# Moving the sums of the spectra's squares from VectorE to GpSimd, and the store and spread load of the sampling offsets to later steps

## The chip, the cores and the metric

The kernel runs on one core of a Trainium2 chip. The metric is the device time of one execution in microseconds (us); lower is better. The engines of the core are named as in the profile: PE (TensorE, matrix products; its weight loads are shown apart as PEld), DVE (VectorE), ACT (ScalarE), POOL (GpSimd) and SP (SyncE, which here only issues transfers). Each of them runs its own instructions in order and waits for the others by semaphores. DMA transfers are issued from the queues of SP, ACT and POOL.

## The reference, cut to what matters

The input is 32 images of 96 channels, 56x56 pixels, float32. Two layers follow each other. The first expands 96 to 576 channels, runs a 3x3 depthwise convolution, weighs the channels by a squeeze and adds a projection back to 96. The second one is a deformable block, and the change lies in it:

```python
mag = jnp.abs(jnp.fft.rfft2(x, norm='ortho'))       # spectrum of the input, |.| per channel
...                                                   # channel weights ca and pixel weights sa from it
y = x * ca * sa
magy = jnp.abs(jnp.fft.rfft2(y, norm='ortho')).mean(1, keepdims=True)
freq_e = jax.image.resize(magy, (b, 1, h, w), method='bilinear')
aux = jnp.concatenate([y, coord, freq_e], 1)
offset = _conv(aux, off_w, off_b, (1, 1))             # 9 taps x (dx, dy) for each pixel
...
sampled = _grid_sample_taps(y, px, py)                # bilinear samples at the shifted places
y_def = jnp.einsum('bcthw,oct->bohw', sampled, def_w.reshape(c, c, 9))
```

So each image needs two spectra of 96 channels (of `x` and of `y`), and each pixel needs nine offsets that become weights of the sampling.

## The kernel before, in words

The first layer's output goes to DRAM image by image (`x1d`). Three pieces of work are interleaved by hand in `layers` and run at the same time for three images: `first(b + 2)`, the expansion and depthwise convolution (`hidden`, its taps are the L262 instructions of DVE); `second(b + 1)`, projection, spectra and attention (`attend`); and the deformable convolution of image b, which goes over seven bands of 8 rows (`NBD`, from L1120 on). `first` and `second` are generators. A band has 17 slots; in each slot `pump()` advances both generators as far as their share of the 119 slots of an image says, and beside it the generator `offsets` of the band after next is advanced by one `yield` for each of the 14 column tiles of the band. "A step" is one such `yield`.

**The spectra** are made by `dft_mag`, which `attend` calls twice for each image: once on `x` (the first spectrum; its resized mean is `fe`), once on `y` (the second; `fy`). In its last loop (L411 to L426) it goes over three groups of channels. For each group PE makes the real and imaginary parts in two PSUM banks (L420), ACT squares both into a tile `sq` of 128x2x2x232 (L423, two instructions), and DVE adds the squares of the two parts into the spectrum tile `s1` (L424, one instruction, 128x464). The pool `sq` has two buffers, so the squares of the third group need the sum of the first one to be done. After the three groups ACT takes the root of all of it in place (L427), and `resized_spectrum` reduces it over the channels on DVE (`m_fe` or `m_fy`, L437; for the second spectrum DVE first weighs it, L436), and PE multiplies that with a small matrix (L440).

**The offsets** are made by `offsets`, one call for each band, two bands ahead. PE convolves (`joint_conv`, L615), DVE copies the 18 offset rows out of PSUM into the tile `at` (L664), POOL stores `at` to a DRAM tile `od` (L668), SP loads `od` back, spread over 112 partitions, as `ht` (L680, 252 KB), and ACT turns `ht` into hat functions `ho` (L686 and L688), which go out to DRAM (`hd`, L690) and come back as the sampling weights `wc` and `wr` (L702, L703), which DVE multiplies (L709) and PE uses (L738). Between these, the base convolution of the band runs (L644), and DVE reduces `at` to the largest offset (L675).

**The order.** The instruction order of PE, ACT, DVE and POOL is made when the program is built, by a list scheduler that has its own estimate of the times and follows the order of the program text as priority. SP's queue is in the order of the program text (`manual_schedule`). An instruction given to `keep_in_program_order` is tied to its place in the text. Other transfers of SP's queue that matter here: `hq<-h2d` (L311, the rows of the first layer for the projection, 784 and 980 KB by turns; the projection's matmuls are L329), `hq<-x1d` (L369, rows for the spectra, twelve of 98 KB for each spectrum), `xt<-in_x` (L213) and `yp<-x1d` (L594). POOL also copies blocks of the image (`ybl`, L720, twice for each half band), weighs the rows for the second spectrum (L373), adds the residual (L476), and issues the transfers L317, L477, L571, L587, L596 and L1060. PE's other lines in what follows: L169 (expansion), L396 (first half of the transform), L724 (transposes of `ybl`), L757 (deformable convolution). The spectrum's rows are put into `s1` by ACT (L403); L649 and L173 are the evacuations of the base convolution and the expansion.

Of the kernel before, what the change touches and what calls it, by code (L numbers as in the profile page):

```python
# [7 lines left out]
FP = mybir.dt.float32  # L8
# [20 lines left out]
NOFF, NTAP = 18, 9  # L29
# [8 lines left out]
NTX = W // TS  # L38
NTH = NTX // 2
TP = TS * TS  # L40
# [22 lines left out]
NQB = 8  # L63
# [54 lines left out]
def bank(p):  # L118
    return p["mm"].tile([128, 512], FP, name="mm")
# [182 lines left out]
def project_rows(p, half):  # L302

    return p["hq"].tile([128, (NCH - 1, len(UNITS) - NCH + 1)[half], EW], FP, name=f"hq{half}")
# [39 lines left out]
def dft_mag(nc, p, src, gate=None):  # L344

    w = p["w"]
    hwc = src.rearrange("c (h w) -> h c w", h=H)
    s1 = p["s1p"].tile([2 * WX, NP, 2 * V], FP, name="s1")
    if gate is None:
        parts = p["sq"].tile([2 * WX, 2, NPB * V], FP, name="sq")[: 2 * H, :, : NG * W].rearrange("p k (g w) -> p k g w", g=NG)
    x2s = []
    for i in range(2):  # L360
        rows = project_rows(p, i).rearrange("p u n -> p (u n)")[: 2 * H, : NG // 2 * CG * WX].rearrange("h (c w) -> h c w", w=WX)
        nc.vector.memset(rows[:, :, W:], 0.0)
        x2s.extend(rows[:, g * CG : (g + 1) * CG] for g in range(NG // 2))

    def load(g):
        if g < NG:
            for half in range(2):
                c0 = half * C // 2 + g * CG
                nc.sync.dma_start(x2s[g][half * H : (half + 1) * H, :, :W], hwc[:, c0 : c0 + CG])  # L369

    def weigh(g):
        if gate is not None and g < NG:
            nc.gpsimd.tensor_tensor(x2s[g][:, :, :W], x2s[g][:, :, :W], gate.unsqueeze(1).to_broadcast([2 * H, CG, W]), ALU.mult)  # L373

    def sums(g):
        sq = bank(p)[: 2 * H, : CG * W].rearrange("h (c w) -> h c w", c=CG)
        nc.scalar.activation(sq, x2s[g][:, :, :W], AF.Square)
        for k, t in enumerate((x2s[g][:, :, :W], sq)):
            nc.vector.tensor_reduce(parts[:, k, g], t.rearrange("h c w -> h w c"), AX.X, ALU.add)

    if gate is None:
        yield
    for g in range(3):
        load(g)
    yield
    if gate is not None:
        yield
    weigh(0)
    weigh(1)
    yield  # L390
    if gate is not None:
        yield
    for g in range(NG):
        pt = bank(p)
        for i in range(CG // 2):
            nc.tensor.matmul(pt[:, i * 4 * V : (i + 1) * 4 * V],  # L396
                             x2s[g][:, 2 * i : 2 * i + 2, :].rearrange("h c w -> h (c w)"), w["FU"],
                             start=True, stop=True)
        if gate is None:
            sums(g)  # L400
        weigh(g + 2)
        load(g + 3)
        nc.scalar.copy(s1.rearrange("p (h q) u -> p h q u", h=2)[:, :, g * CG // 2 : (g + 1) * CG // 2],  # L403
                       pt[:, : 2 * CG * V].rearrange("p (q h u) -> p h q u", h=2, u=2 * V))
        yield
    if gate is None:
        p["sums"] = p["sp"].tile([2 * H, 2, W], FP, name="sums")
        nc.vector.tensor_reduce(p["sums"], parts.rearrange("p k g w -> p k w g"), AX.X, ALU.add)
    mag = s1[:, :, :V]
    n = NQB * V  # L410
    pairs = mag.rearrange("p (r q) u -> p r q u", r=2)  # L411
    for q0 in range(0, NP // 2, NQB):
        sq = p["sq"].tile([2 * WX, 2, 2, n], FP, name="sq")
        pts = bank(p), bank(p)
        for part, first, second in ((0, (0, 0), (1, V)), (1, (0, V), (2, 0))):
            for t, (g, u0) in enumerate((first, second)):
                for r, k in ((0, 0), (1, 1), (0, 1), (1, 0)):
                    rows = slice(r * WX, r * WX + W)
                    q1 = k * NP // 2 + q0
                    nc.tensor.matmul(pts[r][k * WX : (k + 1) * WX, part * n : (part + 1) * n].rearrange("p (q u) -> p q u", q=NQB),  # L420
                                     w["GV"][rows, g], s1[rows, q1 : q1 + NQB, u0 : u0 + V], start=(t == 0), stop=(t == 1))
        for r, pt in enumerate(pts):
            nc.scalar.activation(sq[:, r].rearrange("p k n -> p (k n)"), pt[:, : 2 * n], AF.Square)  # L423
        nc.vector.tensor_tensor(pairs[:, :, q0 : q0 + NQB], sq[:, :, 0].rearrange("p r (q u) -> p r q u", q=NQB),  # L424
                                sq[:, :, 1].rearrange("p r (q u) -> p r q u", q=NQB), ALU.add)
        yield  # L426
    nc.scalar.activation(mag, mag, AF.Sqrt)  # L427
    p["magnitude"] = mag
# [18 lines left out]
def attend(tc, p, b, x, h2d, pooled, x1, given=False):  # L447
# [32 lines left out]


    yield from dft_mag(nc, p, x1)
    mag = p["magnitude"]

# [89 lines left out]


    yield from dft_mag(nc, p, x1, sa)
    yield
    yield from resized_spectrum(nc, p, p["magnitude"], "fy", cx)
# [50 lines left out]
def joint_conv(nc, p, yp, j, hid):  # L629


    w = p["w"]
    pa = bank(p)
    conv3(nc, pa[:, :BW], w["joint"], yp, CJ, j)
    nc.scalar.activation(hid, pa[:DMID, :BW], AF.Relu, bias=w["dg1b"][:DMID])  # L635
    yb = p["yb"].tile([C, BW], FP, name="yb")
    nc.scalar.activation(yb[BC:], pa[OFF0 + QC :, :BW], AF.Identity, bias=w["cv"]("base_b")[BC:])
    yield yb, pa[OFF0 : OFF0 + NOFF, :BW]
    pb = bank(p)
    for k in range(NTAP):  # L640
        dy, dx = divmod(k, 3)
        r0 = j * RB + dy + PD - 1
        for i in range(2):
            nc.tensor.matmul(pb[i * BC : (i + 1) * BC, : BW // 2].rearrange("p (h w) -> p h w", h=RB // 2), w["base"][:, k],  # L644
                             yp[:C, r0 + i * RB // 2 : r0 + (i + 1) * RB // 2, dx + PD - 1 : dx + PD - 1 + W],
                             start=(k == 0), stop=(k == NTAP - 1))
    yield
    for i in range(2):
        nc.scalar.activation(yb[:BC, i * BW // 2 : (i + 1) * BW // 2], pb[i * BC : (i + 1) * BC, : BW // 2], AF.Identity,  # L649
                             bias=w["cv"]("base_b")[:BC])  # L650
    yield


def offsets(nc, p, yp, j, top, hid, ybs, hds, defer):

    w = p["w"]
    joint = joint_conv(nc, p, yp, j, hid)
    yb, pa = next(joint)  # L660
    ybs.append(yb)
    at = p["off"].tile([NOFF, NTX, 2, TP], FP, name="at")
    for s in range(2):
        nc.vector.tensor_copy(at[:, :, s].rearrange("o t (r c) -> o t r c", r=TS),  # L664
                              pa[:, s * BW // 2 : (s + 1) * BW // 2].rearrange("o (r t c) -> o t r c", r=TS, t=NTX))
    yield
    od = p["dp"].tile([NTX, 2, NOFF, TP], FP, name="od")
    nc.gpsimd.dma_start(od.rearrange("t s o p -> o (t s) p"), at.rearrange("o t s p -> o (t s) p"))  # L668
    yield
    next(joint)  # L670
    yield
    next(joint)
    yield
    next(joint, None)
    nc.vector.tensor_reduce(top, at.rearrange("o t s p -> o (t s p)"), AX.X, ALU.max, apply_absolute_value=True)  # L675
    for _ in range(4):
        yield
    ht = p["ht"].tile([SB * NTX, 4, KP], FP, name="ht")
    src = od.rearrange("t s o p -> t (s o p)").unsqueeze(0).to_broadcast([SB, NTX, 4 * KP])
    nc.sync.dma_start(ht.rearrange("q n k -> q (n k)"), src)  # L680
    for _ in range(6):
        yield

    def hats():
        ho = p["ht"].tile([SB * NTX, 2, 2, KP], FP, name="ho")
        p["tc"].keep_in_program_order(nc.scalar.activation(  # L686
            ho.rearrange("q x s n -> q s x n"), ht.rearrange("q (s x) n -> q s x n", s=2), AF.Abs, bias=w["blk"]))
        nc.scalar.activation(ho, ho, AF.Relu, bias=w["one"], scale=-1.0)  # L688
        hd = p["dp"].tile([2, 2, SB, NTX, KP], FP, name="hd")
        nc.scalar.dma_start(hd.rearrange("x s i t n -> (i t) (x s) n"), ho.rearrange("q x s n -> q (x s) n"))  # L690
        hds.append(hd)

    defer(hats)
# [259 lines left out]
def layers(tc, a, dp, x1d, zd, stats, far):  # L953
# [8 lines left out]
    with ExitStack() as ctx:  # L962
# [127 lines left out]
        def find(n):  # L1090
            if n % 2 == 0:
                hids.append(p["hid"].tile([2 * NS, BW], FP, name="hid"))
            hid = hids[n // 2][n % 2 * NS : n % 2 * NS + DMID]
            return offsets(nc, p, yp, bands[n][1], top[:, n % NBD : n % NBD + 1], hid, ybs, hds,
                           lambda hats: later.append((slot + 2, hats)))
# [420 lines left out]
```

## Time and profile before

| | us |
|---|---|
| three runs | 9002.55, 9001.68, 8979.61 |
| median | 9001.68 |
| the profiled execution | 8993.57 |
| its span, from the first to the last instruction | 8991.8 |
| PE busy, share of the span | 8180.0, 91% |
| DVE busy | 7174.8, 80% |
| ACT busy | 5380.8, 60% |
| POOL busy | 2600.4, 29% |
| mean granted clock of TensorE over the span | 0.940 |

How to read it: the first 450 us and the last 310 us hold the filling and the normalisation of the outputs; between them the profile repeats itself with one image every 263 us (the root L427 of the first spectrum starts at 3966.6 and the next one at 4229.5). Busy time is a sum over stages. PE's granted clock is either full or half in the records of this trace; a row of the window view gives its mean over a stretch. In the wait view a row names who waited, for whom, the sum of the waits, how many there were, and the longest. In the timeline a bracket gives the idle time before an instruction and what ended it.

### The profile page before, as it was taken

What the parts mean: (1) busy time and instruction counts of PE and PEld (TensorE: products, weight loads), DVE (VectorE), ACT (ScalarE), POOL (GpSimd) and SP (SyncE); (2) the same over time, 40 slices, a digit from 0 to 9 for tenths busy, and PEclk for the clock granted to TensorE, in tenths of its full rate; (3) what the DMA queues carried; (4) which work ended last, traced back from release to release, by engine and by line L of the source; (5) the groups of instructions that cost most, each with busy time, mean ns of one, the idle gap of its engine ahead of it and who ended that gap; (6) DMA issues with size and microseconds to landing.
All of it is one profiled execution on the core that took longest, in us unless ns stands there. A gap on an engine that the chain in (4) does not pass through costs nothing. (4 is left out here: it accounts for less than half of the span.)

```text
span 8991.8 us, 137403 instructions
## 1 busy us (share of the span) xinstructions
PE 8180.0 (91%) x52406; PEld 5185.1 (58%) x52406; DVE 7174.8 (80%) x6821; ACT 5380.8 (60%) x10486; POOL 2600.4 (29%) x2608
## 2 busy tenths in 40 slices
PE   5899999999999999999999999999999999999960
PEld 3456565666656656665666666566566656666640
DVE  7688888888888888888888888888888888887333
ACT  2356666666666666666666666666666666666553
POOL 0133233333323332332332333233333323332210
PEclk9889999999999999999999999999999999999985
DMA  2356666666666666666666666666666666666669
GB/s 80 109 144 167 164 167 164 164 155 155 169 167 167 169 163 150 159 164 167 169 167 160 153 159 166 168 167 168 164 151 162 166 166 168 168 165 146 130 189 417
DMA packets 1068756, 1486.47 MB, mean 165 GB/s; under 512 B 590190, under 2 KB 839838, under 8 KB 1055806
## 3 DMA queue, kind: packets, MB, share of 16 engines
q1 hardware_dynamic: 858995, 985.20, 46.7%
q10 hardware_dynamic: 153803, 329.80, 10.2%
q0 software_dynamic: 55296, 162.60, 6.7%
q8 instruction: 420, 6.88, 0.4%
q14 instruction: 242, 1.98, 0.1%
HBM read 1064.29 MB, written 412.65 MB: 164 GB/s over the span
## 5 line engine op out<-in xcount | busy, mean ns | idle before, releaser
L262 DVE SCALAR_TENSOR_TENSOR acch<-hp,w,acch 128x1512 f32<-128x1512 f32 (+1 forms) x2250 | 4348.3, 1933 | 38.3
L615 PE MATMUL mm<-yp,c_jointW 104*128 104x448 f32 x4032 | 1655.9, 562 | 1.0 <-DMA yp<-fqd 1.0
L720 POOL COPY ybl<-yp 96x448 f32<-96x448 f32 x896 | 1035.1, 1183 | 1541.2 <-PE mm L724 1541.0
L757 PE MATMUL pd<-v,c_def 128*96 128x224 f32 (+1 forms) x6272 | 1429.6, 375 | 53.8 <-DVE z L796 29.0
L757 PEld LDWEIGHTS pd<-v,c_def 128*96 128x96 f32 (+1 forms) x6272 | 1039.5, 173 | 349.1 <-issue 74.5
L615 PEld LDWEIGHTS mm<-yp,c_jointW 104*128 104x128 f32 x4032 | 768.0, 194 | 758.2 <-issue 724.7
L738 PE MATMUL mm<-wc,yt 64*96 64x144 f32 x12544 | 1086.6, 302 | 115.7 <-ACT yb L649 44.8
L738 PEld LDWEIGHTS mm<-wc,yt 64*96 64x96 f32 x12544 | 845.6, 165 | 430.2 <-issue 193.2
L173 ACT ACTIVATE hp<-mm,sh,inv 128x392 f32<-128x392 f32 (+2 forms) x1216 | 812.0, 672 | 461.9 <-PE mm L169 416.4
L169 PE MATMUL mm<-xt,w 96*128 96x392 f32 (+3 forms) x2688 | 1056.8, 527 | 34.4 <-DMA xt<-in_x 33.4
L742 ACT COPY v<-mm 96x288 f32<-96x288 f32 (+1 forms) x2688 | 1003.6, 442 | 126.9 <-PE mm L738 81.4
L329 PE MATMUL mm<-hq,w3s 128*96 128x392 f32 x2048 | 796.8, 536 | 99.2 <-DMA hq<-h2d 92.4
L709 DVE TENSOR_TENSOR wc<-wc,wr 128x1008 f32<-128x1008 f32 x448 | 562.7, 1256 | 365.8 <-DMA wr<-hd 338.6
L644 PE MATMUL mm<-yp,c_base0W 96*64 96x224 f32 x8064 | 827.3, 357 | 0.0
L668 POOL DMA_DIRECT2D od<-at x224 | 185.6, 829 | 2217.9 <-DVE at L664 1515.6
L749 ACT COPY v<-v 32x448 f32<-32x448 f32 x1344 | 755.2, 562 | 29.7
L644 PEld LDWEIGHTS mm<-yp,c_base0W 96*64 96x64 f32 x8064 | 554.0, 135 | 275.4 <-issue 61.5
L726 ACT COPY yt<-mm 128x384 f32<-128x384 f32 (+1 forms) x896 | 350.5, 439 | 544.3 <-PE mm L724 543.8
L635 ACT ACTIVATE hid<-mm,c_dg1b 50x448 f32<-50x448 f32 x224 | 140.6, 628 | 862.9 <-PE mm L615 853.6
L329 PEld LDWEIGHTS mm<-hq,w3s 128*96 128x96 f32 x2048 | 339.1, 174 | 453.1 <-issue 311.0
L222 ACT ACTIVATE acch<-acch,sh,inv 128x1568 f32<-128x1568 f32 x288 | 488.3, 1695 | 180.3 <-DVE acch L262 167.0
L476 POOL TENSOR_TENSOR o<-o,xc 96x392 f32<-96x392 f32 x256 | 374.3, 1462 | 738.9 <-ACT o L339 737.3
(194 smaller groups left out, 9146.8 us busy)
## 6 DMA issues: line engine op xcount, KB each, us to landing
h2d<-acch ACTq DMA_DIRECT2D x288, 784.0 KB
wc<-hd SPq DMA_DIRECT2D x896, 252.0 KB
wr<-hd SPq DMA_DIRECT2D x448, 504.0 KB
hq<-h2d SPq DMA_DIRECT2D x128, 980.0 KB
hq<-h2d SPq DMA_DIRECT2D x128, 784.0 KB
hq<-x1d SPq DMA_DIRECT2D x768, 98.0 KB
ht<-od SPq DMA_DIRECT2D x224, 252.0 KB
hd<-ho ACTq DMA_DIRECT2D x224, 252.0 KB
```

The source lines that it names most:

```text
L169: nc.tensor.matmul(pt[p0 : p0 + w1.shape[1], : rows * W], w1, xts[hf][:, r0 * W : (r0 + rows) * W], start=True, stop=True)
L173: nc.scalar.activation(h1[lo:hi, row0 : row0 + rows, 1 : 1 + W], pt[lo:hi, : rows * W].rearrange("p (h w) -> p h w", h=rows), AF.Silu, bia ...
L262: nc.vector.scalar_tensor_tensor(acc[:, lo:hi], win, wk, acc[:, lo:hi], ALU.mult, ALU.add)
L329: nc.tensor.matmul(pts[half][:C, :EW], w3s[:, ch], hq, start=(i == 0), stop=False)
L615: nc.tensor.matmul(view, weights[:, k], yp[:channels, r0 : r0 + RB, dx + PD - 1 : dx + PD - 1 + W], start=(k == 0), stop=(k == NTAP - 1))
L644: nc.tensor.matmul(pb[i * BC : (i + 1) * BC, : BW // 2].rearrange("p (h w) -> p h w", h=RB // 2), w["base"][:, k], yp[:C, r0 + i * RB // 2 ...
L709: p["tc"].keep_in_program_order(nc.vector.tensor_tensor(wc, wc, wr, ALU.mult))
L720: nc.gpsimd.tensor_copy(yb[:, :, s], blocks)
L738: nc.tensor.matmul(pt[k][:C, (t - lo) * KP : (t - lo + 1) * KP], yt[ps, t], s[ps, t * KP : (t + 1) * KP], start=True, stop=True)
L742: nc.scalar.copy(v[:C, :, lo:hi, k].rearrange("c k t p -> c t k p"), pt[k][:C, : (hi - lo) * KP].rearrange("c (t k p) -> c t k p", t=hi - ...
L749: nc.scalar.copy(v[C:, 1 + 2 * i : 3 + 2 * i], v[i * QC : (i + 1) * QC, KA:])
L757: nc.tensor.matmul(out.rearrange("c q (t x) -> c t q x", x=TS), p["w"]["def"][ks, k], v[ks, k].rearrange("c t s (r x) -> c t (s r) x", r=T ...
```

## The change

Three edits. In `dft_mag` the sum L424 is given to POOL instead of DVE. In `offsets` the store of `od` is issued two steps later, after the matmuls of the base convolution, and it is tied to its place in the text; and the load of `ht` is issued three steps later, with three steps fewer behind it, so that the hat functions keep their step.

```diff
         for r, pt in enumerate(pts):
             nc.scalar.activation(sq[:, r].rearrange("p k n -> p (k n)"), pt[:, : 2 * n], AF.Square)
-        nc.vector.tensor_tensor(pairs[:, :, q0 : q0 + NQB], sq[:, :, 0].rearrange("p r (q u) -> p r q u", q=NQB),
+        nc.gpsimd.tensor_tensor(pairs[:, :, q0 : q0 + NQB], sq[:, :, 0].rearrange("p r (q u) -> p r q u", q=NQB),
                                 sq[:, :, 1].rearrange("p r (q u) -> p r q u", q=NQB), ALU.add)
...
     yield
+    yield
+    next(joint)
+    yield
     od = p["dp"].tile([NTX, 2, NOFF, TP], FP, name="od")
-    nc.gpsimd.dma_start(od.rearrange("t s o p -> o (t s) p"), at.rearrange("o t s p -> o (t s) p"))
-    yield
-    next(joint)
-    yield
+    p["tc"].keep_in_program_order(
+        nc.gpsimd.dma_start(od.rearrange("t s o p -> o (t s) p"), at.rearrange("o t s p -> o (t s) p")))
     next(joint)
     yield
     next(joint, None)
     nc.vector.tensor_reduce(top, at.rearrange("o t s p -> o (t s p)"), AX.X, ALU.max, apply_absolute_value=True)
-    for _ in range(4):
+    for _ in range(7):
         yield
     ht = p["ht"].tile([SB * NTX, 4, KP], FP, name="ht")
     src = od.rearrange("t s o p -> t (s o p)").unsqueeze(0).to_broadcast([SB, NTX, 4 * KP])
     nc.sync.dma_start(ht.rearrange("q n k -> q (n k)"), src)
-    for _ in range(6):
+    for _ in range(3):
         yield
```

The built order of the changed program against that of the one before: PE's instructions stand in the same order throughout. ACT's differ in four short places, two around the first images and two at the end of the program. DVE loses the 192 sums, and some of its other instructions change places with their neighbours. On POOL, for each image in the repeating part, the three sums of the first spectrum stand between two pairs of L720, and those of the second one between a pair of L720 and a store L668; the stores L668 keep their places among POOL's other instructions. In SP's queue, for each image, two of the seven loads L680 change places with other transfers: one goes behind the `hq<-h2d` load of 784 KB that followed it, one behind the six `hq<-x1d` loads that followed it.

More of the change, by code (lines that the diff above doesn't have):

```diff
@@ L666, in offsets @@
     yield
-    od = p["dp"].tile([NTX, 2, NOFF, TP], FP, name="od")
-    nc.gpsimd.dma_start(od.rearrange("t s o p -> o (t s) p"), at.rearrange("o t s p -> o (t s) p"))
     yield
@@ L671, in offsets @@
     yield
+    od = p["dp"].tile([NTX, 2, NOFF, TP], FP, name="od")
+    p["tc"].keep_in_program_order(
+        nc.gpsimd.dma_start(od.rearrange("t s o p -> o (t s) p"), at.rearrange("o t s p -> o (t s) p")))
     next(joint)
```

## The prediction

> **What bounds the kernel now.** I read the page's first two parts, then the windows, the waits, and the timeline of one image.
>
> ```profile
> PE 8180.0 (91%) x52406; PEld 5185.1 (58%) x52406; DVE 7174.8 (80%) x6821; ACT 5380.8 (60%) x10486; POOL 2600.4 (29%) x2608
> ...
> 450.00:8500.00 8050.00, 7664.57 (x49733) 4863.86 (x49731) 6710.92 (x6136) 5027.34 (x9886) 2511.44 (x2487) 0.96 0.65 162
> ...
> 4063.00:4079.00 16.00, 12.45 (x61) 9.24 (x62) 14.43 (x14) 10.73 (x20) 2.92 (x5) 0.57 0.49 142
> ...
> 4157.00:4161.00 4.00, 3.02 (x5) 1.52 (x6) 3.93 (x3) 2.35 (x4) 2.45 (x2) 0.57 1.12 295
> ```
>
> In the repeating part (the second row) PE is busy 95% of the time: it is the bound, and only its pauses can be won. A pause costs twice: after it the granted clock (the number before the last two) is half for a while. It is 0.57 from 4063 to 4079, and the eight L329 at 4157.98 below take 4.29 us where eight just before took 2.87. From the trace's clock records and the stretches in which neither PE nor its weight load ran I counted, from 450 to 8500 us: 379 us idle, 713 us of half clock. Idle time plus half of the half-clock time in which PE worked is 695 us of loss. Three places of each image hold most of it (means over 28 to 29 images):
>
> - first spectrum, before L440: 2.0 us idle, 3.5 half clock, loss 3.7
> - second spectrum, L724 to L440: 4.6, 10.1, loss 8.9
> - one L329 in the second band: 3.1, 5.1, loss 5.3
>
> ```profile
> ACT s L427 <- DVE s L424: 110.4, 31, 4.6
> ...
> PE mm L329 <- DMA hq<-h2d: 92.4, 30, 4.1
> ...
> ACT sq L423 <- DVE s L424: 72.4, 25, 5.7
> ...
> PE acc L440 <- DVE m_fe L437: 60.3, 31, 2.2
> ...
> PE mm L738 <- ACT yb L649: 44.8, 29, 1.9
> ...
> PE mm L738 <- ACT hp L173: 43.6, 31, 1.9
> ```
>
> The waits name them; each comes about once an image. The timeline tells why, for the second spectrum, the L329 and the first spectrum:
>
> ```profile
> 4058.41 0.64 DVE L424 TENSOR_TENSOR s<-sq 128x464 f32<-128x464 f32 x1
> ...
> 4059.15 1.01 ACT L423 ACTIVATE sq<-mm 128x464 f32<-128x464 f32 x2 [5.46 <-DVE s L424]
> ...
> 4064.36 1.41 ACT L427 ACTIVATE s<-s 128x1392 f32<-128x1392 f32 x1 [2.90 <-DVE s L424]
> ...
> 4063.28 0.77 PE L724 MATMUL mm<-c_ident,ybl 96*128 96x96 f32 x7 [2.08 <-DVE at L664]
> ...
> 4066.60 0.79 PE L738 MATMUL mm<-wc,yt 64*96 64x144 f32 x2 [1.89 <-ACT yb L649]
> ...
> 4068.59 1.27 PE L738 MATMUL mm<-wc,yt 64*96 64x144 f32 x6 [1.20 <-ACT hp L173]
> ...
> 4141.85 0.66 SPq L680 DMA_DIRECT2D ht<-od  x1
> ...
> 4144.75 9.08 SPq L311 DMA_DIRECT2D hq<-h2d  x2
> ...
> 4157.98 4.29 PE L329 MATMUL mm<-hq,w3s 128*96 128x392 f32 x8 [3.72 <-DMA hq<-h2d]
> ...
> 3969.52 2.56 DVE L437 TENSOR_REDUCE m_fe<-s 128x29 f32<-128x1392 f32 x1
> ...
> 3972.22 0.35 PE L440 MATMUL acc<-c_RT,m_fe 128*29 128x112 f32 x2 [2.00 <-DVE m_fe L437]
> ```
>
> The first sum of the second spectrum, whose squares were ready at 4043.9, waits until 4058.4 in DVE's queue behind seven L262. ACT stands behind it twice (5.46, then 2.90), and PE behind ACT.
>
> **The change, part by part.**
>
> *Length of a sum on POOL.* No row shows it. Nearest is L476 on POOL: 1.00 us at least for 392 elements, 1.63 on average beside a L262; L373 (448) averages 2.5 beside a L262. By element that is 1.2 to 2.6 us for 464; I take 1.9, the contended L476, which has the same two plain operands, against 0.624 on DVE. Beside POOL DVE slows: 1343 L262 without a POOL tensor instruction average 1.82 us, 332 wholly covered by one 2.14, so each sum costs DVE about 0.3 and gives 0.62 back.
>
> [...]
>
> *Second spectrum.* POOL is idle from 4045.6 to 4063.4 (L720 ends, the store L668 waits 17.8 us for `at`). The first two sums run from 4045.6 to 4049.4. The third squares then wait only for PE's L420 (ends 4054.1), end at 4055.1; sum until 4057.0; root L427 until 4058.4; L649 follows PE's L644 (ends 4057.7), table load 1.28 and L173 until 4061.3. PE needs them after 4064: the waits of 1.89 and 1.20 go. What is late next is DVE: `at` (L664) comes 1.3 earlier for two sums gone and 0.6 later for slowed L262, so L724's 2.08 becomes 1.4; then L675, L436 and L437 follow without the third sum (0.62) and without the 1.47 that L436 waited for the root, so `m_fy` is ready at 4067.4 instead of 4070.0, while PE comes at 4065.0 and waits 2.4. Idle 5.4 to 3.8, half clock 13.7 to about 7: 4.6 won. In every second image L724 does not wait (4325: waits of 0.86, 1.51, 0.93, half clock 10.2); there the same reckoning leaves one wait of 0.85 and wins 7.4. I take 5.5: 30 images, 165 us.
>
> *First spectrum.* DVE had reached the third sum early and waited 2.79 for the squares; without the sums it comes to L437 before the root is done (3967.97), so `m_fe` starts 1.5 earlier. The third sum on POOL starts at 3963.9 and has until 3966.59, where ACT starts the root after its table load: 2.7 us, enough for 1.9, barely for 2.6. Idle 2.0 to 0.5, half clock mostly gone: 2.8 times 30 = 84 us. If a sum takes longer than 2.7, each further us goes to the root one for one. ACT's own gain at L427 is nothing here. POOL's L720 pair behind the sums (3967.36, waiting for PE's L724) isn't touched.
>
> *The load of `ht`, three steps later.* SP's queue is in order. In the second band `ht` now goes out behind the 784 KB `hq` (4144.75) instead of before it (4141.85). By the records half of the 16 engines carry `ht`; on those the last transfer before it ended at 4152.0 to 4153.0, `ht` then took until 4154.9 to 4156.0, and `hq` landed last, at 4157.85, which ended PE's 3.72; on the other eight `hq` was there at 4153.0. With `hq` first it lands some 2.3 earlier: wait 3.1 to 0.8 on average, half clock mostly gone: 4.1 times 30 = 123 us. `ht` itself lands later by the 32 `hq` packets an engine carries, at 66 to 96 ns, 2.1 to 3.1 us, so ACT's wait at L686 (3.68 there) grows to about 6. What covers this: PE next needs ACT's L339 (behind L686 and L688) at L738, behind 18 L615, some 10 us after this L329. Without that cover 2.1 to 3.1 us an image would come back, 63 to 93 us. In another band `ht` goes behind six `hq<-x1d` (issued 3991 to 3998); it landed at 3997 and will at about 4001; L686 reads it at 4008.9: nothing. Those six go out 0.7 us earlier, also nothing (PE's waits for them are 15 us in all).
>
> *The store of `od`, two steps later, tied.* POOL's order keeps it between the same neighbours but the sums; it waits for `at` in nearly all bands, so it starts when it did. Behind the third sum (4057) it is free before `at` (4063). Zero; a step is 263/119 = 2.2 us, so two unhidden ones would be 4.4 per band for `ht`, which had 5 us of room in the tightest band (issued 4035.9, read 4040.9) and 12 to 24 in the others. No wait is added on SP: the load waits for the store as before.
>
> *Sum.* 165 + 84 + 123 = 372. Once PE runs ahead it will find next waits (DVE has 83% of the repeating part to do); I take 0.8 of it, 298: 8993.6 - 298 = 8696, with the median 8 us above the profiled execution 8704, said as 8700. 0.3% (27 us) is about what the runs' spread can tell from no change.
>
> [...]
>
> **The rivals.**
>
> 1. *Idle time is won, half clock stays*, because smaller pauses remain (2.4 and 1.4 at the second spectrum). Then 1.5, 2.0 and 2.3 an image, 30 times: 174; 8820. For it: pauses of 2 us trip the clock. Against: most of the remaining ones are under 1.
> 2. *At L329 another wait takes the place*: the weight load of the same L329 is put down to ACT's L688, 108.8 us, 29 times. If that, not `hq`, holds it, the later `ht` makes it worse by 2.1 to 3.1: +80, and the rest 0.8 of 249: 8993.6 + 80 - 199 = 8875. Against: the matmul's own wait names `hq`, and the bank it needs was read by L742, long done.
> 3. *Slower: DVE is held by POOL for each whole sum.* At the second spectrum DVE then is 3 x 1.9 later and 3.4 earlier, `m_fy` 2.3 late: with the clock 4 lost, 120 in all; at the first 5.7 later against 4.7 earlier (2.79 and three sums), with the clock 1.5, 45; with 123 won at L329 it ends at 9040. It decides when a sum holds DVE for more than 1.3 us. For it: L720 stretches from 0.55 to 7.0 us at the worst, L373 from 1.13 to 4.6. Against: L262's averages.
> 4. *Nothing moves*: the sums are covered and `ht` is read late anyway. 8995. Against: the waits' releasers.
>
> **How the numbers follow.** Main case 0.60 (8590 to 8800: all of the 372 and some more, or half), rival 1 0.14, rival 2 0.12, rival 3 0.08, rival 4 0.06. Faster: 0.60 + 0.14 + 0.12 = 0.86; same 0.06; slower 0.08. The range takes in rivals 1 and 2: 8590 to 8900.
>
> **What would show it.** The waits of L427 and L423 for the sum fall from 183 us to under 80; L738's for L649 and L173 (88) nearly vanish; L329's for `hq` falls to about 30; L440's for `m_fy` grows, `m_fe` falls; L686's for `ht` doubles to about 200; the mean granted clock rises from 0.940 to about 0.96; DVE's busy time falls by 60 to 120, POOL's rises by 230 to 500. Wrong it would be if L427's wait stays because POOL's sums take over 2.7 us, or if PE's pauses move to `at` and `m_fy` in full.

## The result, and the profile after

The change made the kernel slower: 9048.75 us in the median of five runs (9031.94 to 9059.03), against 9001.68 for the kernel before (five runs, 8973.15 to 9009.64). The ratio is 1.0064, 95% interval 1.0048 to 1.0080. The forecast was 8700. The profiled execution of after took 9059.03 us, its span 9057.2.

Where after is read its own line numbers stand: from the load of `ht` on they are one higher, so before's L680, L686, L709, L724, L738, L757 and L796 are L681, L687, L710, L725, L739, L758 and L797; the store L668 is L672.

The page and the windows of after, for the lines shown of before:

```profile
PE 8175.3 (90%) x52406; PEld 5193.5 (57%) x52406; DVE 7184.4 (79%) x6629; ACT 5393.5 (60%) x10486; POOL 2902.8 (32%) x2800
...
450.00:8500.00 8050.00, 7594.93 (x49179) 4826.58 (x49179) 6697.70 (x5918) 4995.48 (x9790) 2781.44 (x2644) 0.95 0.64 161
```

VectorE lost 192 instructions, but its busy time did not fall (7174.8 to 7184.4). The groups by line tell most of why, first before, then after:

```profile
L262 DVE SCALAR_TENSOR_TENSOR acch<-hp,w,acch 128x1512 f32<-128x1512 f32 (+1 forms) x2250 | 4348.3, 1933 | 38.3
...
L424 DVE TENSOR_TENSOR s<-sq 128x464 f32<-128x464 f32 x192 | 119.8, 624 | 66.1 <-ACT sq L423 65.9
```

```profile
L262 DVE SCALAR_TENSOR_TENSOR acch<-hp,w,acch 128x1512 f32<-128x1512 f32 (+1 forms) x2250 | 4456.4, 1981 | 141.4 <-ACT hp L173 103.8
...
L424 POOL TENSOR_TENSOR s<-sq 128x464 f32<-128x464 f32 x192 | 279.6, 1459 | 413.2 <-ACT sq L423 413.2
```

The sums took 119.8 us on VectorE; its L262 became 108 us longer and also waits 104 us more for `hp`. Three waits of before that the prediction does not show, then the waits of after:

```profile
PE acc L440 <- DVE m_fy L437: 30.0, 31, 6.3
...
PE pd L757 <- DVE z L796: 29.0, 25, 3.0
...
PE mm L724 <- DVE at L664: 19.1, 13, 2.3
```

```profile
ACT ho L687 <- DMA ht<-od: 173.5, 34, 7.3
...
PE pd L758 <- DVE z L797: 115.6, 26, 6.1
...
DVE acch L262 <- ACT hp L173: 103.8, 29, 4.1
...
PE acc L440 <- DVE m_fy L437: 72.8, 30, 5.6
...
PE acc L440 <- DVE m_fe L437: 71.1, 31, 2.5
...
PE mm L329 <- DMA hq<-h2d: 62.2, 31, 4.2
...
PE mm L725 <- DVE at L664: 57.2, 28, 5.7
...
ACT s L427 <- POOL s L424: 24.1, 28, 2.1
```

The waits that the change was aimed at did shrink: the root's for the sum from 110.4 to 24.1, L329's for `hq` from 92.4 to 62.2, and of L738's (L739) for `yb` and `hp`, 88 us, 3 are left. In their place PE waits longer for VectorE: for `z` (29.0 before), `at` (19.1), `m_fy` (30.0), `m_fe` (60.3).

With the prediction's measure (idle time of PE and its weight load, plus half of the half-clock time in which PE worked, 450 to 8500 us) I counted the loss of each place in every profile. The fourth place is new: 10 to 45 us after ACT starts the second band's `ho`. What is left of the steady part when the loss is taken off agrees within 25 us over all profiles, so the loss says where the time went to about that; a single profile's place moves by some 10 us.

| us of loss | first spectrum | second spectrum | L329 | `z` place | all |
|---|---|---|---|---|---|
| before | 107 | 258 | 148 | 70 | 695 |
| after | 141 | 233 | 70 | 203 | 778 |

L329 gave 78, the second spectrum 25; the first cost 34 and the place of `z` 133. The timeline of after shows that place (the transfer's issue, the hat functions, L329, then VectorE and PE behind it):

```profile
3922.57 0.67 SPq L681 DMA_DIRECT2D ht<-od  x1
...
3935.06 0.77 ACT L687 ACTIVATE ho<-ht,c_blk 112x576 f32<-112x576 f32 x1 [5.37 <-DMA ht<-od]
...
3933.68 2.84 PE L329 MATMUL mm<-hq,w3s 128*96 128x392 f32 x8 [2.07 <-DMA hq<-h2d]
...
3956.58 1.53 DVE L710 TENSOR_TENSOR wc<-wc,wr 128x1008 f32<-128x1008 f32 x1 [3.47 <-DMA wr<-hd]
3958.03 6.09 DVE L262 SCALAR_TENSOR_TENSOR acch<-hp,w,acch 128x1568 f32<-128x1568 f32 x3
3964.15 0.68 DVE L797 SCALAR_TENSOR_TENSOR z<-pd,c_cvec,yb 96x448 f32<-96x448 f32 x1
...
3964.98 1.03 PE L758 MATMUL pd<-v,c_def 96*96 96x224 f32 x2 [4.84 <-DVE z L797]
```

PE won at L329 (2.07 here, 3.72 in the image of before that the prediction shows) and stood still 31 us later for 4.84. L758 writes the one bank `pd` that L797 reads; L797 stands in VectorE's queue behind three L262 and L710; L710 waits for the weights `wr`, which come from `hd`, that from `ho`, that from `ht`. The medians over 28 images show the chain, with L335 (PE, right behind L329's burst) as a mark of how far PE is:

| us from the issue of `od`'s store | before | after |
|---|---|---|
| `ho` starts on ACT | 28.1 | 30.3 |
| `hd` has landed | 41.3 | 40.6 |
| PE's L335 | 45.6 | 42.7 |
| L709 (L710) starts | 52.4 | 51.7 |
| L757 (L758) writes `pd` | 60.3 | 59.9 |

PE came to L335 2.9 us sooner, and to L758 0.4 sooner. The chain from `od` to `z` is what PE waits for there, and nothing in the change made it shorter: its end hardly moved, and what PE had won it lost there.

### The profile page after: what moved, and what is told of

Read it like the earlier page. It is cut to its first block, busy times and chain, and to the rows that moved or that the text cites. A ratio compares the mean times of both kernels' runs of the same rounds, so it can differ in the third digit from the quotient of the medians.

```text
span 9057.2 us, 137476 instructions
## 1 busy us (share of the span) xinstructions
PE 8175.3 (90%) x52406; PEld 5193.5 (57%) x52406; DVE 7184.4 (79%) x6629; ACT 5393.5 (60%) x10486; POOL 2902.8 (32%) x2800
## 5 line engine op out<-in xcount | busy, mean ns | idle before, releaser
L262 DVE SCALAR_TENSOR_TENSOR acch<-hp,w,acch 128x1512 f32<-128x1512 f32 (+1 forms) x2250 | 4456.4, 1981 | 141.4 <-ACT hp L173 103.8
L615 PE MATMUL mm<-yp,c_jointW 104*128 104x448 f32 x4032 | 1679.6, 568 | 10.1 <-DMA yp<-fqd 10.1
L758 PE MATMUL pd<-v,c_def 128*96 128x224 f32 (+1 forms) x6272 | 1468.8, 382 | 142.7 <-DVE z L797 115.6
L721 POOL COPY ybl<-yp 96x448 f32<-96x448 f32 x896 | 1048.3, 1198 | 1204.9 <-PE mm L725 1204.8
L758 PEld LDWEIGHTS pd<-v,c_def 128*96 128x96 f32 (+1 forms) x6272 | 1062.2, 176 | 449.8 <-issue 116.9
L615 PEld LDWEIGHTS mm<-yp,c_jointW 104*128 104x128 f32 x4032 | 776.6, 196 | 784.2 <-issue 747.4
L739 PE MATMUL mm<-wc,yt 64*96 64x144 f32 x12544 | 1056.9, 300 | 20.8 <-DVE sq L379 6.7
L739 PEld LDWEIGHTS mm<-wc,yt 64*96 64x96 f32 x12544 | 834.2, 164 | 317.3 <-issue 199.1
L173 ACT ACTIVATE hp<-mm,sh,inv 128x392 f32<-128x392 f32 (+2 forms) x1216 | 810.7, 673 | 344.8 <-PE mm L169 290.5
L710 DVE TENSOR_TENSOR wc<-wc,wr 128x1008 f32<-128x1008 f32 x448 | 566.6, 1265 | 412.5 <-DMA wr<-hd 385.1
L329 PE MATMUL mm<-hq,w3s 128*96 128x392 f32 x2048 | 749.7, 510 | 63.6 <-DMA hq<-h2d 62.2
L672 POOL DMA_DIRECT2D od<-at x224 | 186.7, 834 | 1908.3 <-DVE at L664 1292.6
L329 PEld LDWEIGHTS mm<-hq,w3s 128*96 128x96 f32 x2048 | 323.0, 166 | 395.2 <-issue 367.5
```

The costliest lines, as they stand in the source:

```text
L173: nc.scalar.activation(h1[lo:hi, row0 : row0 + rows, 1 : 1 + W], pt[lo:hi, : rows * W].rearrange("p (h w) -> p h w", h=rows), AF.Silu, bia ...
L262: nc.vector.scalar_tensor_tensor(acc[:, lo:hi], win, wk, acc[:, lo:hi], ALU.mult, ALU.add)
L329: nc.tensor.matmul(pts[half][:C, :EW], w3s[:, ch], hq, start=(i == 0), stop=False)
L615: nc.tensor.matmul(view, weights[:, k], yp[:channels, r0 : r0 + RB, dx + PD - 1 : dx + PD - 1 + W], start=(k == 0), stop=(k == NTAP - 1))
L710: p["tc"].keep_in_program_order(nc.vector.tensor_tensor(wc, wc, wr, ALU.mult))
L721: nc.gpsimd.tensor_copy(yb[:, :, s], blocks)
```

## The experiments

Ratios are to the kernel before, run beside it on the same chip, with 95% intervals.

**Sums alone.** Theory A, after the two traces: the weights that come late cost the time. Theory B: the slowed VectorE does.

```diff
-        nc.vector.tensor_tensor(pairs[:, :, q0 : q0 + NQB], ...
+        nc.gpsimd.tensor_tensor(pairs[:, :, q0 : q0 + NQB], ...
```

> Only the sums go to GpSimd; the offsets' store and load stay as before. Counted in the trace of after against before, per image place: first spectrum +34 us of loss in all, second spectrum -25, one L329 in the second band -78, the place 10 to 45 us behind that band's ho (L758 waiting for z) +133. Theory A (late weights): the +133 belongs to the later ht, not to the sums, so the sums alone cost 34 - 25 = +9 us: 8995 to 9035, ratio 0.999 to 1.004, loss at the z place near before's 70 us, L262 busy some 100 us more than before. Theory B (slowed VectorE): the slowed L262 and z's place one instruction later make z late; then the sums alone cost over 120 us: ratio 1.013 or more, z place over 180 us.

Measured: 9089.57, ratio 1.0102 (1.0087 to 1.0118). Neither theory has it right: 93 us over before is more than A allows and less than B's 120, and the `z` place, at 76 us, is near before's. The second spectrum lost 323 instead of 258. A row of this run's waits, and then the timelines of GpSimd and ACT:

```profile
ACT s L427 <- POOL s L424: 251.2, 31, 12.4
```

```profile
4101.26 0.84 POOL L668 DMA_DIRECT2D od<-at  x1 [14.81 <-DVE at L664]
4102.11 1.17 POOL L424 TENSOR_TENSOR s<-sq 128x464 f32<-128x464 f32 x1
...
4103.32 1.40 ACT L427 ACTIVATE s<-s 128x1392 f32<-128x1392 f32 x1 [9.87 <-POOL s L424]
```

The third sum stands behind the store of `od`, which waits 14.81 us for `at`; the root waits 9.87 for the sum. The store's move is no detail, as the run with sums and store below shows.

**The offsets alone.** Store and load are moved as in the change, the sums stay on VectorE.

> Only the offsets' store and load are moved; the sums stay on VectorE. Theory A: wins 78 us at L329, loses about 133 at the place where PE's L758 waits for z, because the weights come later: 9040 to 9070, ratio 1.004 to 1.008; L758's wait for z about 100 us in all against 29 before. Theory B: only the win is left: 8915 to 8940, ratio 0.990 to 0.993, L758's wait for z near 29 us.

Measured: 9030.44, 1.0045 (1.0029 to 1.0061). `z` place 151, L329's 92, all 730; PE's waits:

```profile
PE pd L758 <- DVE z L797: 77.3, 25, 6.2
...
PE mm L329 <- DMA hq<-h2d: 62.0, 31, 4.5
```

That is theory A's mechanism; the ratio is at the lower end of its range, and the time 10 us below it. From `od`'s store PE needs 44.0 us to L335 and about 60 to L758.

**The later load in one band of seven.**

```diff
-    for _ in range(4):
+    for _ in range(7 if j == 1 else 4):
         yield
     ht = p["ht"].tile(...)
...
-    for _ in range(6):
+    for _ in range(3 if j == 1 else 6):
```

> The kernel before, with the load of ht three steps later in the second band of each image alone; store and sums as before. VectorE's order is that of before. Theory A: all that the offsets' move does lies in this band: L329's place falls to 75 to 95 us, z's rises to 130 to 170; the ratio is that of the offsets alone (1.0045) within 0.002. Rival C (z is late because the move exchanges instructions on VectorE, or because of the loads of other bands): z's place stays at 60 to 80, ratio 0.990 to 0.995.

Measured: 9033.86, 1.0038 (1.0022 to 1.0054), the same as the run before within the intervals; L329's place 87, `z`'s 156. PE's waits:

```profile
PE pd L757 <- DVE z L796: 85.3, 28, 5.9
...
PE mm L329 <- DMA hq<-h2d: 61.9, 31, 4.2
```

VectorE's order here is that of before, so no exchange of instructions makes `z` late: the load of `ht` in the second band does, and the store's move and the loads of the other bands cost nothing that can be measured.

**The weights taken from the band before**, to cut the chain; once on the offsets alone, once on the kernel before. What these two kernels leave out is that a band uses its own weights.

```diff
-                loads.append(weights_load(nc, p, hds[n], m))
+                loads.append(weights_load(nc, p, hds[max(n - 1, 0)], m))
```

> As the offsets alone, but the weights wc and wr of a band are loaded from the hd of the band before, which lies ready: L710 no longer waits for the chain ht, ho, hd (the part left out is that a band uses its own weights). The instructions and their order on VectorE and TensorE stay those of the offsets alone. Theory A: the z place falls from about 200 us to under 60, the win at L329 stays: some 140 us less than the offsets alone, 8890 to 8930, ratio 0.988 to 0.992. Theory B: wr is not what holds z, so the time equals that of the offsets alone within 0.2%.

> The kernel before, with the weights of a band loaded from the hd of the band before. Theory A: of the 70 us lost at the z place some 30 to 60 go, and nothing else: 8940 to 8980, ratio 0.993 to 0.998; the wait of L329 for hq stays near 92 us. Theory B: no change, within 0.2%.

Measured: 8954.84, 0.9950 (0.9934 to 0.9965), and 8922.14, 0.9908 (0.9891 to 0.9924). Both theories forecast a gain and both missed its size. SP's waits, first on the offsets alone, then on the kernel before, show that the edit did not do in the second band what it was made for:

```profile
SPq L703 <- DMA hd<-ho: 372.9, 31, 13.7
```

```profile
SPq L702 <- DMA hd<-ho: 382.4, 32, 13.6
```

Without the edit these waits were 1598.9 us (134 times) and 1570.4 (133). The one that is left, 12 us in each image, stands ahead of the second load of `wc` in the second band: in 29 of 30 images of the first run and in all 30 of the second this load waits on a semaphore that the write of the same band's own `hd` signals, and goes out when that write has landed (3899.01 and 3899.03 in one image), though it reads the `hd` of the band before. So the chain was cut in the other bands and not there. Only the first load of `wc` went out earlier, by 11 us; the last one, `wr`, did not (0.19 us after L335 on the offsets alone, without the edit 1.59 ahead of it). L709 (L710) then started 0.8 us sooner against L335 on the offsets alone and 1.9 sooner on the kernel before, and the `z` place fell from 151 to 129 and from 70 to 28. On the kernel before VectorE's waits for `wr` fell from 338.6 to 272.2 us, most of that in this place. So weights that come earlier do take loss from the `z` place. The whole gain there, 75 us in the medians, is more than the place held; the counted loss fell by 43 in all, and where the rest lies is open.

**The reverse: the load of `ht` one step earlier in the second band**, ahead of the loads of `wc` and `wr` in SP's queue (by the page's sizes 1008 KB, not the 756 of the expectation: two of 252 and one of 504).

```diff
-    for _ in range(4):
+    for _ in range(3 if j == 1 else 4):
...
-    for _ in range(6):
+    for _ in range(7 if j == 1 else 6):
```

> The kernel before, with the load of ht in the second band of each image one step earlier, so that in SP's queue it goes ahead of the weights wc, wc, wr (756 KB) instead of behind them: the reverse of the change, in one band. Theory A (the chain ht, ho, hd, wr, L710, z, L757 is what holds PE there): ho and wr come 2 to 4 us earlier against PE, z's place falls from 70 us to 20 to 45, L329's place stays at 130 to 155: ratio 0.992 to 0.997. Rival C (z is held by VectorE's order, not by the weights): ratio 0.998 to 1.002, z's place 60 to 80.

Measured: 9011.69, 1.0016 (1.0002 to 1.0030). At the place the mechanism is A's: `z`'s place fell from 70 to 16, L329's from 148 to 118, and PE's wait for `z` from 29.0 to 4.2 us. But the time did not fall. PE's waits:

```profile
PE mm L329 <- DMA hq<-h2d: 78.1, 30, 5.6
PE mm L738 <- DVE sq L379: 69.5, 31, 2.3
PE mm L738 <- ACT yb L649: 46.7, 29, 1.9
```

A wait of 17.6 us in all before, L738 for a bank that VectorE's reduction L379 has read, is 69.5 now, and L396 waits 20.8 for the same line, which it did not do before. VectorE pauses there for 0.2 us in 26 (3934 to 3961): what PE wins ahead of this stretch, it meets in it.

**With the reductions earlier too.** The squares and reductions L377 and L379 of a group are made one step earlier.

```diff
+    if gate is None:
+        sums(0)
     for g in range(NG):
...
-        if gate is None:
-            sums(g)
+        if gate is None and g + 1 < NG:
+            sums(g + 1)
```

> The kernel before with the load of ht one step earlier in the second band (which took the loss at z from 70 to 16 us and gave it back at L738, whose bank VectorE's L379 freed 69 us too late), and the first spectrum's squares and reductions L377, L379 one step earlier. Theory: the bank comes free in time, L738's wait for sq falls from 69 us to under 15, z stays under 30: ratio 0.987 to 0.994. Rival (VectorE has no room left in that stretch, so that its next result is late instead): 0.997 to 1.002.

Measured: 8985.30, 0.9975 (0.9962 to 0.9989): a little faster than the kernel before and than the run above, and within the rival's range, not the theory's. The waits say the same (lines two higher):

```profile
PE mm L398 <- DVE sq L379: 58.8, 28, 3.1
...
PE mm L740 <- DVE sq L379: 22.6, 17, 1.4
```

L738's (L740) wait for `sq` fell from 69.5 to 22.6 us, but that of the transform's first half (L398, L396 before) for the same reductions rose from 20.8 to 58.8. VectorE has little room in that stretch.

**Sums and store without the load's move**: the change, with `range(4)` and `range(6)` back.

> The change without the move of the load: sums on GpSimd, the store two steps later and tied, the load of ht where it was. Theory: with the sums alone (ratio 1.010) GpSimd's third sum of the second spectrum stood behind the store, which waits for at: L427 waited 251 us for the sum, that place lost 323 us instead of 258. With the store behind the sums this goes: L427's wait for the sum under 50 us, the place 225 to 250 us. The first spectrum stays at 130 to 145, z's place near 75, L329's near 145. Ratio 1.000 to 1.005. Rival: the store's place does nothing and the slowed VectorE makes the loss; then as the sums alone, 1.008 to 1.012.

Measured: 8999.48, 0.9995 (0.9981 to 1.0008). The store behind the sums takes back the whole 1% of the sums alone, as the theory said (the root's wait for the sum is 26.5 us, not 251.2), and the sums win nothing. So without the load's move the change is as fast as before. Waits of this run:

```profile
PE acc L440 <- DVE m_fe L437: 71.0, 31, 2.5
PE mm L329 <- DMA hq<-h2d: 67.5, 23, 3.9
PE acc L440 <- DVE m_fy L437: 67.3, 28, 6.3
PE mm L725 <- DVE at L664: 65.2, 28, 6.3
...
ACT s L427 <- POOL s L424: 26.5, 28, 2.1
```

L329's wait is 67.5 here, with the load at its old step, hardly more than after's 62.2: that row alone does not measure the place. In the count of loss, half clock included, the place stays within some 15 us of before's 148.

**Only the second spectrum's sums**, with the store behind them.

```diff
+        (nc.vector if gate is None else nc.gpsimd).tensor_tensor(pairs[...
```

> As the sums and the store, but only the second spectrum's three sums on GpSimd, the first spectrum's on VectorE. Theory: the first spectrum is back at about 107 us of loss, the second stays at 225 to 250: 0.3 to 0.5% better than with all sums, ratio 0.996 to 1.000. Rival (VectorE slowed by GpSimd wherever a sum runs): half of the slowing is left, ratio 1.000 to 1.003.

Measured: 8992.49, 0.9989 (0.9973 to 1.0004): not to be told from before. The first spectrum is back at 105. With 96 sums on GpSimd instead of 192, L262 is still 83.6 us longer than before (4431.9), 0.87 per sum; the first spectrum's sums cost it only 0.1 each, since VectorE mostly waits for `hp` then (104.7 us, 29 times, in the run with sums and store). This run with the earlier load of `ht` as well:

> The second spectrum's sums on GpSimd, the store two steps later and tied, and the load of ht one step earlier in the second band instead of three later. Theory: z's place under 30 us as with the earlier load alone, the second spectrum at 235 to 255, L738's wait for sq stays at 60 to 75: ratio 0.996 to 1.001. Rival (the two effects add): 0.990 to 0.995.

9000.43, 0.9991 (0.9978 to 1.0004), as the theory said, with two places just past their bounds: `z` at 33, the second spectrum at 234, and the wait for L379 at 65.5.

**VectorE relieved at the second spectrum.** L436, 1.6 us of VectorE ahead of `m_fy`, is left out (fy is then not scaled), in before and in the sums with the store.

```diff
-    if scale is not None:
-        nc.vector.tensor_tensor(mag, mag, scale..., ALU.mult)
```

> The kernel before without L436, VectorE's product of the second spectrum with cx ahead of m_fy (1.6 us an image; left out, so that fy is not scaled). VectorE reaches L437 1.6 us earlier in each image. In before PE's L440 waits for m_fy only 18 us in all, the waits of L738 for yb and hp stay: 0 to 30 us won, ratio 0.996 to 1.000.

> The sums on GpSimd and the store behind them, the load where it was, and L436 left out as in the run above. Theory (at the second spectrum the win of the root was taken back by VectorE, which comes to m_fy too late): L440's wait for m_fy, 67 us there, falls by 1.6 us an image to about 20, with half clock behind it 50 to 75 us less than with L436: ratio 0.991 to 0.995. Rival (the root and the third sum still set the end of m_fy, or another wait takes the place): no more is won than by the same edit on before, ratio 0.996 to 1.000.

Measured: 8967.69, 0.9958 (0.9944 to 0.9972), on before; 8993.52, 0.9993 (0.9980 to 1.0006), with the sums on GpSimd, where 0.991 to 0.995 was expected. The step is right and its worth is not: the wait for `m_fy` fell from 67.3 to 27.3 and the second spectrum's loss from 247 to 189, but PE ran into the next one (lines two less):

```profile
PE mm L723 <- DVE at L662: 61.9, 29, 4.7
...
PE mm L613 <- DMA yp<-fqd: 40.7, 17, 4.5
...
PE acc L438 <- DVE m_fy L435: 27.3, 24, 4.8
```

The joint convolution (L615, L613 here) now waits 40.7 us (7.0 with L436) for the row that is made from `m_fy` and comes back through DRAM. That the same edit won more on before (35 us in the medians, just over the bound) has no explanation here; the wait for `m_fy` was 30.0 there, not the 18 of the expectation.

**The whole change but for the one load**: in the second band `ht` is loaded at its old step, in the other six three steps later.

```diff
-    for _ in range(7):
+    for _ in range(4 if j == 1 else 7):
...
-    for _ in range(3):
+    for _ in range(6 if j == 1 else 3):
```

> The whole change, but in the second band of each image the load of ht stays at its old step; in the other six bands it is three steps later. If that one load makes all of the loss, with the sums or without: ratio 0.998 to 1.001, the z place at 70 to 95 us. Rival (the sums and the other bands' loads together cost the 0.2% by which the change is worse than the offsets alone): 1.001 to 1.004.

Measured: 9002.33, 1.0025 (1.0014 to 1.0037). The places are near those of the sums with the store: 131, 233, 125 at L329, 98 at `z` (203 with the whole change), 724 in all. So here too that one load makes the `z` place. On the 0.25% the ratio is in the rival's range and clear of no change, but the run leaves it open: beside it the kernel before took 8979.03 in the median, some 20 us less than beside the earlier ones (8996.66 to 9002.83), and in microseconds this run and the sums with the store (8999.48) are the same.

**What the reductions are worth alone, and all three together.**

> The kernel before with only the first spectrum's squares and reductions one step earlier, the load of ht where it was. If the gain of 0.25% of the run with both needs both (the chain to z first, then VectorE's L379): ratio 0.998 to 1.002. If the reductions alone are worth it: 0.995 to 0.998.

> The load of ht one step earlier in the second band, the first spectrum's reductions one step earlier, and the second spectrum's sums on GpSimd with the store behind them. The sums were worth 0 to 0.25% alone: ratio 0.994 to 0.998; rival: VectorE, slowed by 0.87 us a sum, gives it back as everywhere, 0.997 to 1.000.

Measured: 8978.22, 0.9989 (0.9977 to 1.0001), and 8954.88, 0.9965 (0.9952 to 0.9979), within the first range of each expectation. The reductions alone are worth nothing that can be measured. With the earlier load and the second spectrum's sums the kernel is 24 us faster than before: the best version of these runs that computes everything. Its waits (lines two to three higher) still name VectorE:

```profile
PE acc L442 <- DVE m_fy L439: 77.4, 30, 7.0
PE mm L329 <- DMA hq<-h2d: 70.8, 29, 5.2
PE acc L442 <- DVE m_fe L439: 59.8, 31, 2.0
PE mm L398 <- DVE sq L379: 58.4, 25, 3.8
```

## Why the prediction was wrong, step by step

Of the three gains forecast, 165 us at the second spectrum, 84 at the first and 123 at L329 (0.8 of the sum was taken), the count of loss has 25, -34 and 78; the `z` place, put at nothing, has -133.

**Where it was right.** Which waits the change removes (the root's and the squares' for the sum fell from 183 to 26 us), and that L329's place goes by the order in SP's queue. The wait for `m_fy` was forecast at 2.4 us an image and is 72.8 / 30 = 2.4, in part by luck, since `at` ahead of it came otherwise than forecast. Of its signs these did not come: L329's wait at about 30, a falling wait for `m_fe`, a clock of 0.96 (0.939), and VectorE's busy time lower by 60 to 120 (it is 10 higher). A sum on GpSimd takes 1.46 us on average (1.2 in the first spectrum, 1.7 in the second), within the bounds of 1.2 to 2.6. The store costs nothing that could be measured where it stands behind the sums.

**The step that failed first: "What covers this" at the load of `ht`.** The prediction saw that `ht` lands 2.1 to 3.1 us later, followed it to ACT's L686 and L339, found PE's need of L339 10 us away, and stopped. It did not follow `ho` on through `hd`, `wr` and L709 to `z` and L757, whose wait for `z` stood in the list of before (29.0 us, 25 times): a chain with no room left. By the table of medians the later start of `ho` (2.2 us) was made up when `hd` landed, and L757 came when it had come before; so what failed is that PE could keep its gain at L329. It reached L335 2.9 us sooner and L757 only 0.4 sooner. Where the load moved and the sums did not, 56 and 61 us were won at L329 and 81 and 86 lost at `z`, within the 63 to 93 that the prediction gave for a lost cover, though half clock is part of it; with the sums beside it the place lost 133, and why so much more is not shown. The gain at L329 was 78 of 123: the wait for `hq` fell by 1.1 us an image, not 2.3.

**Second failed step: "each sum costs DVE about 0.3 and gives 0.62 back".** At the second spectrum a sum costs VectorE 0.87, so three make it 0.75 us later instead of earlier. Then `at`, forecast 0.7 us earlier, does not come in time: PE waits for it in nearly all images (57.2 us, 28 times), where before it waited in 13, and the "7.4 won in every second image" is empty. Of 5.5 us an image, 0.4 to 0.9 came. The prediction had measured the mean of L262 wholly covered by GpSimd (2.14 against 1.82), which mixes in long GpSimd instructions that were themselves held up (in before L720 takes 0.55 to 7.0 us, L373 1.13 to 4.6): 103 of these 332 L262 lie inside a single GpSimd instruction of 2.3 us or more and take only 1.83. The timelines of VectorE and GpSimd in after show single cases:

```profile
4088.02 6.76 DVE L262 SCALAR_TENSOR_TENSOR acch<-hp,w,acch 128x1568 f32<-128x1568 f32 x2
```

```profile
4088.09 1.06 POOL L721 COPY ybl<-yp 96x448 f32<-96x448 f32 x2
4089.12 1.17 POOL L424 TENSOR_TENSOR s<-sq 128x464 f32<-128x464 f32 x1
4091.97 1.17 POOL L424 TENSOR_TENSOR s<-sq 128x464 f32<-128x464 f32 x1 [1.68 <-ACT sq L423]
```

Two L262 take 3.69 us undisturbed (1.843 each, the mean in after of those of 128x1568 with no GpSimd instruction beside them); these take 3.07 more, for 3.40 us of GpSimd beside them. An L262 with one whole sum in it and nothing else is 0.97 longer for a sum of 1.16 (two cases in after). In these three cases 82 to 90% of the GpSimd time is lost to VectorE, so the premise of the third rival, that a sum holds VectorE for its whole length, is much nearer to them than the 0.3 of the prediction was. In the rows above it is the L262 that is held and not the sum: the sum at 4089.12, which started while the first L262 ran, took 1.17 us like the other, and that L262, with the two copies L721 beside it as well, 3.93 instead of 1.84.

**Third: the first spectrum.** "Without the sums it comes to L437 before the root is done": VectorE did not, because it needs `hp` first. The timeline of VectorE and then PE in after:

```profile
4009.54 2.17 DVE L262 SCALAR_TENSOR_TENSOR acch<-hp,w,acch 128x1568 f32<-128x1568 f32 x1 [4.03 <-ACT hp L173]
...
4014.81 2.54 DVE L437 TENSOR_REDUCE m_fe<-s 128x29 f32<-128x1392 f32 x1
...
4017.50 0.35 PE L440 MATMUL acc<-c_RT,m_fe 128*29 128x112 f32 x2 [2.36 <-DVE m_fe L437]
```

In before the third sum waited 2.79 us for the third squares; now the L262 behind it waits 4.03 for an L173 that ACT runs right after the same squares. The wait moved by one instruction and L437 came no sooner: 84 us forecast, a loss of 11 (sums and store) to 34 (after).

**The factor 0.8** for "next waits" was the weakest number. The 372 us were sums of waits at places that all lie in one loop with VectorE, which has 83% of that part to do, with hardly a pause over 26 us in the one stretch looked at above. The real share was below zero.

**The rivals.** The third one forecast 9040 by a VectorE held at the sums and 123 won at L329. The time was near (9049) by luck, its reason not: the sums with the store came out even, and the place of L329 with what hangs on it made the loss. What remains open: whether the change is more than the sum of its parts (1.0064, against 1.0045 for the offsets and 0.9995 for the rest). With the whole change PE is 1.3 us further ahead at L335 than with the offsets alone, and the `z` place 52 us worse, which fits the chain but is not shown to follow from it; the run without that load leaves 0.25% that its neighbours do not show.

## What to carry to other kernels

When a transfer is issued later, follow its data to the last engine that waits for it, not to the first instruction that has slack, and look in the list of waits for that last one: a wait that is already there, however short, says that there is little cover (29.0 us in 25 waits for `z` in before, 115.6 in 26 in after). A wait that is removed on one engine is a gain only if the engine that the waiting one meets next has room (here the root's wait for the sum fell by 86 us, and PE's for `m_fy` rose by 43); a run that makes that chain start earlier, and one that takes work from the second engine, show it before the work is done. A run that is meant to cut a chain must be read for whether it did: here a semaphore kept the load behind the very write that it no longer read. And a queue in order decides whether work can be moved to an idle engine: the sums alone cost 1% behind a store that waited, and nothing ahead of it.

## What was not expected of the hardware

A 128x464 sum of two SBUF tiles on GpSimd lengthens the L262 that it falls into by 0.97 us for its own 1.16 (two cases in after that nothing else touches). The write of `hd` in the second band (252 KB in 576-byte packets) takes 11.8 us from issue to landing in before and 9.6 in after (medians of 29 images). In after it starts some 5 us later against PE's L335 and lands only 2 to 3 later: a late start of a transfer was partly made up, and why is not shown. And in after the pauses of 2.4 us before L440 are still followed by half clock: 5.3 us an image at the first spectrum, against 3.5 in before, where the pauses are 2.0 us long. By the trace's clock records half clock begins in the pause, or in the 1.5 us behind its end, in 28 of 30 images in after and in 21 of 30 in before.
